# Folding score matrices with heads and key channels on the partitions, and a preparation with its own order

## The chip, the cores and the metric

The kernel runs on one core of a Trainium2 chip. The metric is device time in microseconds (us), the median of several executions; lower is better. The engines have short names: PE is TensorE (matrix products, with PEld for its weight loads), DVE is VectorE, ACT is ScalarE, POOL is GpSimd, SP is SyncE, which here only issues transfers (DMA).

## The reference

Two transformer-like layers on x of shape (8, 512, 256), fp32. Cut to what matters here:

```python
xn = layernorm(x)
q, k, v = split(xn @ Wq.T), split(xn @ Wk.T), split(xn @ Wv.T)      # 16 heads of 64 channels
k, v = concat(mem_k, k), concat(mem_v, v)                           # 64 memory keys in front
dots = einsum('bhid,bhjd->bhij', q, k) * 64 ** -0.5
dots = einsum('bhij,hk->bkij', dots, pre_proj)                      # heads are mixed
...                                          # causal mask; only the 64 largest of a row are kept
attn = einsum('bhij,hk->bkij', softmax(dots), post_proj)
x = x + (attn @ v) @ Wout.T + bout + fp4_ffn(xn)                    # weights and activations rounded to FP4
xn = layernorm(x)
x = x + conv_mlp(xn) + int4_lora_linear(xn)                         # second layer
```

Because the heads are mixed before the softmax, the score of mixed head k between tokens i and j is xn_i times a fixed matrix M_k times xn_j, with M_k = sum over h of pre_proj[h, k] Wq_h^T Wk_h. The kernel computes the 16 matrices M_k (256 x 256 each, and 256 x 64 each for the memory keys) once; this is the fold of the score matrices.

## The kernel before, in words

There are three stages.

**Preparation** (lines 512 to 648, with `prepare`, L240, and `first_guesses`, L378). It loads the weights over two issuing queues (SP and ACT). For each mixed head k it multiplies Wq on DVE with the column pre_proj[:, k] (L587) and runs, for both halves e of the input channels, eight accumulating products over the 1024 inner channels (L593): 16 x 2 x 8 = 256 products, 320 columns each (256 channels and 64 memory keys). ACT copies each result into `mg` and `mgm` (L597, L598) and squares and sums it (L600) for the variance of the scores. `mg` and `mgm` are copied to DRAM. `first_guesses` turns the sums of squares into a first guess of the 64th largest score for each row: a Newton iteration of six rounds, each with a Tanh on ACT (L447) and a chain of small DVE operations. Wv and Wout are transposed. `prepare` rounds the gate, up and down weights of the first layer's MLP to FP4 (steps in `fp4_steps`, L196, that go back and forth between DVE, ACT and POOL; 128 rows of 256 at a time for gate and up, 704 for down), transposes them, and makes the second layer's weights. The results are stored in DRAM (`wgu_d`, `wd_d`, `w1_d`, `bsum_d`). Nobody wrote down an order for this stage: the framework's scheduler picks it, by the place in the program and by readiness.

**The attention loop** (lines 1256 to 1328). The unit is a group: one of the 8 batches and 64 of its 512 tokens; 64 groups. For a batch `tokens` (L687) loads and normalises x and transposes it to `xnT`. `queries` multiplies rows of a pair of groups with `mgm` (L763) and with `mg` (L792); `scores` (L812) multiplies the result with `xnT` (L832) and puts the scores into a place of the ring, a large SBUF buffer with room for four groups. The memory keys' scores go to DRAM and come back in another layout by DMA (L778, L825). `search` (L976) counts in six rounds how many scores of a row lie above a threshold, half on ACT and half on DVE, and starts with a copy of the first guess (L980). Then come the exact 64th value, the exponentials, the head mixing, the product with v and the output projection. All of these operations are added to a `Plan` with an estimated cost and a due time; `Plan.run` (L106) simulates the engines with these costs and emits the instructions in the resulting order[...].

**The second layer** (lines 1377 to 1566), on a batch at a time: parts `norm1`, `convolve`, `norm2` and `finish`, between them the first layer's MLP (`mlp`) of later batches and the rounding of their activations (`quantised`). The framework's scheduler orders this stage, with what comes earlier in the program ahead. Its loop, in short:

```python
for k in range(EARLY, ahead):
    if k not in live and k > b:
        live[k] = quantised(k)
...
(norm1, convolve, norm2, finish)[part](live[b])
```

Of the kernel before, what the change touches and what calls it, by code (L numbers as in the profile page):

```python
# [8 lines left out]
F32 = mybir.dt.float32  # L9
# [57 lines left out]
def keys(ib):  # L67

    return MEM + RB * (ib + 1)


class Op:


    def __init__(self, eng, cost, fn, deps, after, take, give):
        self.eng, self.cost, self.fn, self.deps, self.after = eng, cost, fn, deps, after
        self.take, self.give = take, give
        self.end = self.due = None


class Plan:
# [8 lines left out]
    def add(self, eng, cost, fn, deps=(), take=(), give=(), after=()):  # L90
        op = Op(eng, cost, fn, [d for d in deps if d is not None], [d for d in after if d is not None], take, give)
        if self.room is None:
            fn()
            op.end = 0.0
        else:
            self.ops.append(op)
        return op

# [7 lines left out]
    def run(self, hop=0.1, near=0.08):  # L106
# [13 lines left out]
        while left:  # L120
# [29 lines left out]
            for u in users.get(op, ()):  # L150
                missing[u] -= 1
                if not missing[u]:
                    ready.append(u)

# [85 lines left out]
def prepare(ctx, tc, a, pool, psum, ident, vt, cb, wgu_d, wd_d, w1_d, bsum_d):  # L240

    nc = tc.nc
# [5 lines left out]
    def scratch():  # L248
        return psum.tile([P, 512], F32, name="pps_t")

    with tc.tile_pool(name="pw", bufs=1) as pw:

        vrow = pw.tile([len(VECS), D], F32, name="vrow")
        for i, n in enumerate(VECS):
            (nc.sync, nc.scalar)[i % 2].dma_start(
                vrow[i : i + 1, :], a[f"L1_attn_{n}"].rearrange("(o d) -> o d", o=1)
            )
        ps = scratch()
        for c in range(DC):
            nc.tensor.transpose(  # L260
                ps[:, c * 16 : c * 16 + len(VECS)], vrow[:, c * P : (c + 1) * P], ident[: len(VECS), : len(VECS)]
            )
        nc.vector.tensor_copy(vt, ps[:, : DC * 16].rearrange("p (c v) -> p c v", v=16)[:, :, : len(VECS)])
        for c in range(DC):
            nc.vector.tensor_tensor(cb[:, c : c + 1], vec("Bp", c), vec("Cp", c), ALU.mult)


        wguT = pw.tile([P, DC, 2, FI], F32, name="wguT")
        for u, n in enumerate(("w_gate", "w_up")):
            for r in range(0, FI, P):  # L270
                m = min(P, FI - r)
                w = pool.tile([P, D], F32, name="wrow")
                nc.sync.dma_start(w[:m], a[f"L0_ffn_{n}"][r : r + m, :])
                q = fp4(nc, pool, w[:m], m, D, "w")
                ps = scratch()
                for e in range(DC):
                    nc.tensor.transpose(ps[:, e * P : e * P + m], q[:, e * P : (e + 1) * P], ident[:m, :m])
                nc.scalar.copy(
                    wguT[:, :, u, r : r + m], ps[:, : DC * P].rearrange("p (e m) -> p e m", m=P)[:, :, :m]
                )  # L280
        nc.sync.dma_start(wgu_d, wguT.rearrange("p e u f -> p (e u f)"))
        wdT = pw.tile([P, FKC, D], F32, name="wdT")
        nc.gpsimd.memset(wdT[96:, FKC - 2 :, :], 0.0)
        for o in range(DC):
            w = pw.tile([P, FI], F32, name="wdrow")
            nc.scalar.dma_start(w, a["L0_ffn_w_down"][o * P : (o + 1) * P, :])
            q = fp4(nc, pw, w, P, FI, "d")
            for c0 in range(0, FKC, 3):
                ps = scratch()
                for c in range(c0, c0 + 3):  # L290
                    at, n = FCH[c]
                    nc.tensor.transpose(ps[:n, (c - c0) * P : (c - c0 + 1) * P], q[:, at : at + n], ident)
                for c in range(c0, c0 + 3):
                    at, n = FCH[c]
                    nc.scalar.copy(wdT[:n, c, o * P : (o + 1) * P], ps[:n, (c - c0) * P : (c - c0 + 1) * P])
        nc.sync.dma_start(wd_d, wdT.rearrange("p c d -> p (c d)"))


        w1 = pw.tile([P, 6, DC, D], F32, name="w1")
        for i, n in enumerate(("Wg", "Wi", "Wfg", "Wfu")):  # L300
            (nc.sync, nc.scalar)[i % 2].dma_start(w1[:, i], a[f"L1_attn_{n}"].rearrange("(c p) f -> p c f", p=P))

        for i, n in ((2, "bfg"), (3, "bfu")):
            ps = scratch()
            for o in range(DC):
                for e in range(DC):
                    nc.tensor.matmul(
                        ps[:, o : o + 1], w1[:, i, e, o * P : (o + 1) * P], vec("beta", e),
                        start=(e == 0), stop=(e == DC - 1),
                    )  # L310
            for o in range(DC):
                nc.vector.tensor_tensor(vec(n, o), vec(n, o), ps[:, o : o + 1], ALU.add)
            for e in range(DC):
                nc.vector.tensor_scalar(w1[:, i, e, :], w1[:, i, e, :], vec("gamma", e), None, ALU.mult)

        fd = pw.tile([P, DC, D], F32, name="fd")
        wo1 = pw.tile([P, DC, D], F32, name="wo1")
        nc.sync.dma_start(fd, a["L1_attn_Wfd"].rearrange("(c p) f -> p c f", p=P))
        nc.scalar.dma_start(wo1, a["L1_attn_Wo"].rearrange("(c p) f -> p c f", p=P))
        fdT = pw.tile([P, DC, D], F32, name="fdT")  # L320
        for e in range(DC):
            ps = scratch()
            for c in range(DC):
                nc.tensor.transpose(ps[:, c * P : (c + 1) * P], fd[:, c, e * P : (e + 1) * P], ident)
            nc.scalar.copy(fdT[:, e, :], ps[:, :D])
        for c in range(DC):
            ps = scratch()
            for e in range(DC):
                nc.tensor.matmul(
                    ps[:, :D], fdT[:, e, c * P : (c + 1) * P], wo1[:, e, :], start=(e == 0), stop=(e == DC - 1)  # L330
                )
            nc.scalar.copy(w1[:, 5, c, :], ps[:, :D])
        bfd = pw.tile([P, DC, P], F32, name="bfd")
        for e in range(DC):
            nc.vector.tensor_copy(bfd[:, e, :], vec("bfd", e).to_broadcast([P, P]))
        psb = scratch()
        for e in range(DC):
            nc.tensor.matmul(psb[:, :D], bfd[:, e, :], wo1[:, e, :], start=(e == 0), stop=(e == DC - 1))
        bsum = pw.tile([P, D], F32, name="bsum")
        b1 = pw.tile([P, D], F32, name="b1")  # L340
        nc.sync.dma_start(bsum, a["L1_attn_bo"].partition_broadcast(P))
        nc.scalar.dma_start(b1, a["L1_ffn_bias"].partition_broadcast(P))
        nc.gpsimd.tensor_tensor(bsum, bsum, b1, ALU.add)
        nc.vector.tensor_tensor(bsum, bsum, psb[:, :D], ALU.add)
        nc.sync.dma_start(bsum_d, bsum)

        w4 = pw.tile([P, DC, D], F32, name="w4")
        nc.sync.dma_start(w4, a["L1_ffn_kernel"].rearrange("(c p) f -> p c f", p=P))
        w4f = w4.rearrange("p c f -> p (c f)")
        mx = pw.tile([P, 1], F32, name="mx")  # L350
        nc.vector.tensor_reduce(mx, w4f, AX.X, ALU.max, apply_absolute_value=True)
        mxa = pw.tile([P, 1], F32, name="mxa")
        nc.gpsimd.partition_all_reduce(mxa, mx, P, bass_isa.ReduceOp.max)
        s4 = pw.tile([P, 1], F32, name="s4")
        nc.vector.tensor_scalar(s4, mxa, 1.0 / 7.0, None, ALU.mult)
        r4 = pw.tile([P, 1], F32, name="r4")
        nc.vector.reciprocal(r4, s4)
        nc.vector.tensor_scalar(w4f, w4f, r4, None, ALU.mult)
        nc.vector.tensor_scalar(w4f, w4f, RNE, None, ALU.add)
        nc.vector.tensor_scalar(w4f, w4f, -RNE, None, ALU.add)  # L360
        nc.vector.tensor_scalar(w4f, w4f, 7.0, -8.0, ALU.min, ALU.max)
        nc.vector.tensor_scalar(w4f, w4f, s4, None, ALU.mult)
        la = pw.tile([P, DC, 16], F32, name="la")
        lb = pw.tile([16, D], F32, name="lb")
        nc.sync.dma_start(la, a["L1_ffn_a"].rearrange("(c p) r -> p c r", p=P))
        nc.scalar.dma_start(lb, a["L1_ffn_b"])
        laT = pw.tile([16, DC, P], F32, name="laT")
        for c in range(DC):
            ps = scratch()
            nc.tensor.transpose(ps[:16, :P], la[:, c, :], ident)  # L370
# [1234 lines left out]
```

## Time and profile before

| | us |
|---|---|
| median of 3 runs | 3159.82 (3157.33 to 3160.18) |
| the profiled execution's own time | 3161.28 |
| its span, first to last instruction | 3159.6 |
| PE busy | 2663.9 (84%) |
| DVE busy | 2451.1 (78%) |
| ACT busy | 2052.7 (65%) |
| POOL busy | 1195.4 (38%) |

The page gives for every engine the time that its instructions took. A share is a mean over stages with different limits, so the stages have to be looked at one by one: the profile can be asked for any stretch of time, for the groups of instructions in it (busy time, mean length of one, and the idle time before them with what ended it), for the waits, and for the instructions in order of time. In such a line an arrow `out<-in` names the buffers, `L593` is a line of the kernel, and `[4.74 <-PE x]` after an instruction is the idle time of its engine before it and what ended that. The products are fp32, and each leaves two records in the trace. The mean granted clock of PE was 0.941 of full speed.

### The profile page before, as it was taken

The page shows a single profiled execution, that of the slowest core. Times are in us where ns is not written, and L with a number is a line of the kernel's source. Part 1 is how long each engine was busy: PE and PEld are TensorE (multiplying, and loading weights), DVE is VectorE, ACT ScalarE, POOL GpSimd, SP SyncE. Part 2 cuts the span into 40 slices and gives each one's busy share as a digit, 9 for nine tenths or more (in the row PEclk, how much of TensorE's full clock was granted, in tenths as well). Part 3 has the DMA queues.
Part 4 walks back from the last instruction along what each step waited for, and adds up shares of the span by engine and source line. Part 5 has one row for each costly group of instructions (what it writes and reads, how often), then busy time and mean ns, then how long its engine had stood idle before and what let it go on. Part 6 is the DMA issues. An engine that isn't in the chain of part 4 may idle for free. (4 is left out here: it accounts for less than half of the span.)

```text
span 3159.6 us, 57876 instructions
## 1 busy us (share of the span) xinstructions
PE 2663.9 (84%) x19096; PEld 2033.2 (64%) x19096; DVE 2451.1 (78%) x7973; ACT 2052.7 (65%) x6036; POOL 1195.4 (38%) x2223
## 2 busy tenths in 40 slices
PE   7938889899989989989898998899986558888887
PEld 4726677677768767776776777677664435555554
DVE  5262899989997988899889898979979567776652
ACT  2233878778778877777887787788787334444432
POOL 2030343534534343443434434344445244344330
PEclk9968999999999999999999999999997779999998
DMA  3021000001000100000010000000010110000000
GB/s 109 1 118 49 19 25 17 18 19 30 18 16 18 33 9 26 24 19 16 22 30 16 17 26 17 18 18 26 22 40 5 59 39 20 21 20 14 7 7 13
DMA packets 114152, 82.30 MB, mean 26 GB/s; under 512 B 79131, under 2 KB 108214, under 8 KB 113078
## 3 DMA queue, kind: packets, MB, share of 16 engines
q1 hardware_dynamic: 105548, 66.27, 7.0%
q10 hardware_dynamic: 8298, 12.28, 1.2%
q8 instruction: 153, 2.51, 0.3%
q14 instruction: 153, 1.25, 0.1%
HBM read 43.63 MB, written 34.87 MB: 25 GB/s over the span
## 5 line engine op out<-in xcount | busy, mean ns | idle before, releaser
L874 ACT ACTIVATE junk<-ring,cur 128x312 int8<-128x312 f32 (+26 forms) x1560 | 869.2, 562 | 107.2 <-POOL cur L927 52.7
L878 DVE SCALAR_TENSOR_TENSOR junk<-ring,cur,two 128x72 int8<-128x72 f32 (+10 forms) x1512 | 823.5, 581 | 80.6 <-POOL cur L980 47.0
L832 PE MATMUL ps_sc<-xnT,tk 128*128 128x8 f32 (+38 forms) x2048 | 554.2, 410 | 74.5 <-ACT ring L838 74.2
L792 PEld LDWEIGHTS ps_mi<-rows,mg 128*128 128x128 f32 x4096 | 488.7, 194 | 46.6 <-issue 27.1
L792 PE MATMUL ps_mi<-rows,mg 128*128 128x128 f32 x4096 | 506.8, 278 | 8.5 <-ACT tk L803 4.9
L832 PEld LDWEIGHTS ps_sc<-xnT,tk 128*128 128x128 f32 x2048 | 344.6, 198 | 220.0 <-ACT ring L838 102.8
L1078 PE MATMUL ps_at<-mixd,ring 128*128 128x128 f32 (+1 forms) x3072 | 421.7, 287 | 55.6 <-POOL mixd L1055 33.2
L1078 PEld LDWEIGHTS ps_at<-mixd,ring 128*128 128x128 f32 (+1 forms) x3072 | 379.6, 189 | 97.9 <-POOL mixd L1055 36.0
L962 DVE SCALAR_TENSOR_TENSOR ring<-ring,kth,e 128x520 f32<-128x520 f32 (+56 forms) x512 | 277.3, 559 | 150.4 <-ACT e L953 147.9
L894 POOL TENSOR_TENSOR cur<-base,raw 128x8 f32<-128x8 f32 x186 | 53.1, 286 | 684.3 <-ACT junk L874 671.7
L874 ACT ACTIVATION_READ_ACCUMULATOR junk<-ring,cur 128x1 f32 x1560 | 304.8, 195 | 0.0
L935 DVE SCALAR_TENSOR_TENSOR y<-ring,cur 128x520 f32<-128x520 f32 (+56 forms) x512 | 293.0, 572 | 6.4
L1102 PE MATMUL ps_y<-at,v 128*64 128x64 f32 (+1 forms) x6144 | 224.2, 226 | 78.4 <-ACT at L1084 76.5
L1102 PEld LDWEIGHTS ps_y<-at,v 128*64 128x64 f32 (+1 forms) x6144 | 197.5, 138 | 132.2 <-ACT at L1084 111.2
L938 DVE MAX8 top<-y 128x8 f32<-128x520 f32 (+56 forms) x512 | 255.3, 499 | 17.6
L1084 ACT COPY at<-ps_at 128x512 f32<-128x512 f32 (+1 forms) x384 | 220.8, 579 | 72.5 <-PE ps_at L1078 71.7
L838 ACT COPY ring<-ps_sc 128x456 f32<-128x456 f32 (+56 forms) x512 | 187.9, 373 | 121.1 <-PE ps_sc L832 118.3
L953 ACT ACTIVATE e<-ring 128x520 f32<-128x520 f32 (+56 forms) x512 | 233.0, 474 | 36.2 <-DVE ring L962 34.7
L803 ACT COPY tk<-ps_mi 128x256 f32<-128x256 f32 x512 | 170.6, 371 | 93.2 <-PE ps_mi L792 93.1
L917 POOL TENSOR_TENSOR by<-gap,minus 128x8 f32<-128x8 f32 x124 | 218.9, 1765 | 9.7
L1055 POOL TENSOR_TENSOR mixd<-mix,rden 128x512 f32<-128x512 f32 x128 | 146.8, 1165 | 96.3 <-DVE rden L1047 58.1
L1450 PE MATMUL ps_gu<-mg,xqT 128*128 128x352 f32 x448 | 153.6, 475 | 5.5 <-ACT hid L1454 5.3
(360 smaller groups left out, 4116.8 us busy)
## 6 DMA issues: line engine op xcount, KB each, us to landing
msd<-scr SPq DMA_DIRECT2D x32, 512.0 KB
ring<-msd SPq DMA_DIRECT2D x512, 32.0 KB
scr<-in_L_attn_x_dram SPq DMA_DIRECT2D x9, 512.0 KB
mg_d<-mg SPq DMA_DIRECT2D x1, 4096.0 KB
att<-o SPq DMA_DIRECT2D x64, 64.0 KB
xb<-in_L_attn_x_dram SPq DMA_DIRECT2D x8, 512.0 KB
x<-att ACTq DMA_DIRECT2D x8, 512.0 KB
out_dram<-ob SPq DMA_DIRECT2D x8, 512.0 KB
```

The lines of the kernel that those rows point to most:

```text
L792: nc.tensor.matmul(ps[:, j * P : (j + 1) * P], mg[:, e, k + j, e2 * P : (e2 + 1) * P], toks(e), start=(e == 0), stop=(e == DC - 1),)
L832: nc.tensor.matmul(ps[:, :ntok], q["tk"][side_of(g)][e][:, b].rearrange("p k i -> p (k i)"), o["xnT"][:, e, :ntok], start=(e == 0), stop=( ...
L874: nc.scalar.activation(junk, src, AF.Sign, bias=thr, scale=-1.0, accum_out=raw[:, b : b + 1])
L878: nc.vector.scalar_tensor_tensor(junk, src, thr, two.to_broadcast([P, src.shape[-1]]), ALU.is_ge, ALU.mult, accum_out=raw[:, b : b + 1],)
L917: eng.tensor_tensor(by, gap[:, 1], minus, ALU.pow)
L935: nc.vector.scalar_tensor_tensor(y, src, cur[:, 0, b : b + 1], src, ALU.is_ge, ALU.subtract, reverse1=True)
L938: nc.vector.max(out=top[:, b, :], in_=y)
L953: nc.scalar.activation(e, src, AF.Exp, scale=1.0 / SMALL)
L962: nc.vector.scalar_tensor_tensor(src, src, kth[:, b : b + 1], e, ALU.is_ge, ALU.mult, accum_out=den[:, b : b + 1])
L1078: nc.tensor.matmul(pt[:n, b * P : (b + 1) * P], s[:, 4 * j + b, col : col + n], w["mix"][j][:, b, :], start=True, stop=True,)
L1084: nc.scalar.copy(ats[c][:n, :, j * 4 * RB : (j + 1) * 4 * RB].rearrange("p k (b i) -> p b k i", i=RB), w.pop(("pt", c, j))[:n].rearrange(" ...
L1102: nc.tensor.matmul(w["py"][j * DH : (j + 1) * DH, q * GR : (q + 1) * GR], vs[c][:n, k * DH : (k + 1) * DH], ats[c][:n, k, :], start=(c == ...
```

## The change

It has four parts.

1. **The fold in two steps.** The 256 channels and 64 memory keys are cut into 20 slices of 16. `bd` holds Wk (and the memory keys) in block-diagonal form, so that one product with 32 stationary columns gives, for two heads and 16 key channels, Wq_h^T Wk_h; four such products fill the 128 partitions of a PSUM bank (8 heads by 16 channels), eight both halves of the heads. After a copy to SBUF, a second product with `kr`, which holds pre_proj (scaled) times a 16 x 16 identity pattern, mixes the heads. The squares are taken by ACT on the whole slice and summed in groups of 16 by DVE.
2. **Preparation in an order of its own.** A class `Straight` records each operation of the preparation with an estimated cost and the dependencies found from the memory it touches; `Plan.tails` gives each the length of the longest chain that follows it as its urgency; `Plan.run` writes the order. All loads are issued by SP. Gate and up rows are rounded together (512 columns, six rounds), in two sets of buffers that the down weights use too. The first batch is loaded, normalised and transposed here. Some small constants move into this plan.
3. **First guesses beside the first scores.** Their operations are added to the attention loop's plan, with scratch space in the ring; the searches of the first eight groups and the fourth group's scores wait for them.
4. **Second layer.** In the loop the part of batch b comes before `quantised(k)`.

The core of the diff:

```diff
+    def tails(self):
+        tail = {}
+        for op in reversed(self.ops):
+            op.due = -(tail.get(op, 0.0) + op.cost) + op.late
+            for d in op.deps + op.after:
+                tail[d] = max(tail.get(d, 0.0), tail.get(op, 0.0) + op.cost + 0.1)
...
+        if eng == "PE":
+            return (0.05 + 0.0007 * n) if what == "transpose" else 0.04 + 0.00175 * n
...
-            for k in range(H):
-                wqk = prep2.tile([P, HC, D], F32, name="wqk")
-                nc.vector.tensor_tensor(
-                    wqk, wq, prc[:, :, k : k + 1].to_broadcast([P, HC, D]), ALU.mult
-                )
-                for e in range(DC):
-                    ps = pps.tile([P, 512], F32, name="pps_m")
-                    for c in range(HC):
-                        nc.tensor.matmul(
-                            ps[:, : D + MEM], wqk[:, c, e * P : (e + 1) * P], wkm[:, c, :],
-                            start=(c == 0), stop=(c == HC - 1),
-                        )
-                    nc.scalar.copy(mg[:, e, k, :], ps[:, :D])
-                    nc.scalar.copy(mgm[:, e, k, :], ps[:, D : D + MEM])
...
-            first_guesses(tc, prep, pps, sq, guess, each, far)
...
+            for j in range(NJ):
+                pa = bank("a")
+                for i in range(2):
+                    for u in range(4):
+                        c = 4 * i + u
+                        r.tensor.matmul(
+                            pa[u * 32 : (u + 1) * 32, i * D : (i + 1) * D], bd[:, c, j].rearrange("p t i -> p (t i)"),
+                            wq[:, c, :], start=True, stop=True,
+                        )
+                ab = both[j % 3]
+                r.vector.tensor_copy(ab, pa)
+                pm = bank("m")
+                for e in range(DC):
+                    for i in range(2):
+                        r.tensor.matmul(
+                            pm[:, e * D : (e + 1) * D], ab[:, i * D + e * P : i * D + (e + 1) * P],
+                            kr[:, i].rearrange("p k i -> p (k i)"), start=(i == 0), stop=(i == 1),
+                        )
+                dst = mg[:, :, :, j * 16 : (j + 1) * 16] if j < 16 else mgm[:, :, :, (j - 16) * 16 : (j - 15) * 16]
+                r.scalar.copy(dst, pm.rearrange("p (e k i) -> p e k i", e=DC, i=16))
+                r.scalar.activation(junk[j % 2], pm, AF.Square)
+                r.vector.tensor_reduce(sqp[:, j], junk[j % 2].rearrange("p (q i) -> p q i", i=16), AX.X, ALU.add)
...
+            prepare(r, a, prep, lambda: bank("t"), ident, vt, cb, wgu_d, wd_d, w1_d, bsum_d, wv)
+            r.sync.dma_start(mg_d, mgf)
+            r.sync.dma_start(mgm_d, mgmf)
+            pl.tails()
+            with tc.manual_schedule(engines={nc.tensor.engine, nc.scalar.engine, nc.vector.engine, nc.gpsimd.engine}):
+                pl.run()
...
+        first_guesses(Straight(nc, pl), new, tot, guess, each, far)
+        guessed = pl.add("none", 0.0, lambda: None, list(pl.ops))
+        due(0, 0.0, 0.8)
...
-                o, xdone = tokens(pl, x_in[b])
+                if b == 0:
+                    o, xdone = o0, [pl.add("none", 0.0, lambda: None, (), ["xnT"])]
+                else:
+                    o, xdone = tokens(pl, x_in[b])
...
-            seen = scores(pl, g, s, q, o, qdone, stored)
+            seen = scores(pl, g, s, q, o, qdone, stored, [guessed] * (n == 3))
...
-            tail = search(pl, g, s, w, seen, EDGE if n < 2 else LAST if n > len(groups) - 5 else ROUNDS)
+            tail = search(pl, g, s, w, seen + [guessed] * (n < NG), EDGE if n < 2 else LAST if n > len(groups) - 5 else ROUNDS)
...
+        (norm1, convolve, norm2, finish)[part](live[b])
         for k in range(EARLY, ahead):
             if k not in live and k > b:
                 live[k] = quantised(k)
...
-        (norm1, convolve, norm2, finish)[part](live[b])
```

## The prediction

> **What bounds the kernel now.** I read the span in stretches first: cut where the score fold starts and ends, where preparation ends, at the first search, and where the second layer begins. Columns: stretch, length, busy time and instructions of each engine, granted clock, DMA share, GB/s.
>
> ```profile
> core 0: us, PE busy (x) PEld busy (x) DVE busy (x) ACT busy (x) POOL busy (x), PEclk, DMA share, GB/s
> 0.00:24.00 24.00, 1.08 (x8) 0.93 (x8) 7.00 (x21) 0.00 (x0) 6.07 (x124) 1.00 0.77 219
> 24.00:166.00 142.00, 140.49 (x514) 98.65 (x515) 52.95 (x72) 47.30 (x205) 15.66 (x14) 1.00 0.09 28
> 166.00:222.00 56.00, 11.84 (x63) 7.57 (x64) 48.81 (x201) 18.78 (x45) 21.20 (x31) 0.58 0.24 98
> 222.00:255.00 33.00, 14.27 (x58) 10.97 (x56) 13.06 (x45) 6.16 (x20) 4.19 (x6) 0.60 0.39 151
> 255.00:302.00 47.00, 47.00 (x259) 33.69 (x259) 0.26 (x1) 16.58 (x41) 1.27 (x4) 0.97 0.16 46
> 302.00:2512.00 2210.00, 1954.88 (x16395) 1565.22 (x16393) 1928.39 (x6926) 1711.51 (x5296) 921.98 (x1924) 0.96 0.07 20
> 2512.00:2557.00 45.00, 0.00 (x0) 0.00 (x0) 20.23 (x45) 10.17 (x19) 20.22 (x10) 0.52 0.47 158
> 2557.00:3159.60 602.60, 494.29 (x1808) 316.18 (x1808) 380.36 (x665) 242.24 (x411) 204.79 (x114) 0.92 0.04 14
> ```
>
> Before 302 us the engines work one after another: loads, then TensorE alone for 142 us, then VectorE alone for 56 us (weight rounding and first guesses), then a 33 us remainder with a token norm, then TensorE alone again while VectorE has 0.26 us of work. From 302 us the loop has PE and DVE at 87 to 88%; the change doesn't touch its instructions. So the gain is read from the front.
>
> Next the groups and waits of those stretches, and single records of the time order, for prices:
>
> ```profile
> L593 PE MATMUL pps_m<-wkm,wqk 128*128 128x320 f32 x512 | 140.3, 438 | 0.8 <-DVE wkm L581 0.8
> DVE junk L878 <- POOL cur L980: 47.0, 1, 47.0
> 254.96 3.15 PE L721 MATMUL ps_mi<-wvT,xnT 128*128 128x512 f32 x4
> 257.95 3.60 PE L763 MATMUL ps_mi<-mgm,rows 128*128 128x512 f32 x8
> 603.69 1.15 PE L1102 MATMUL ps_y<-at,v 128*64 128x64 f32 x32 [3.27 <-ACT at L1084]
> 23.38 0.69 DVE L581 COPY wkm<-pps_t 128x512 f32<-128x512 f32 x1 [0.32 <-PE pps_t L576]
> 39.84 0.68 DVE L351 TENSOR_REDUCE mx<-w 128x1 f32<-128x512 f32 x1
> 166.29 0.23 DVE L393 COPY fg_tot<-pps_t 128x64 f32<-128x64 f32 x1 [16.75 <-PE pps_t L391]
> 215.62 0.21 DVE L464 TENSOR_TENSOR guess<-guess,fg_f 128x64 f32<-128x64 f32 x1
> 2539.27 2.06 ACT L191 ACTIVATE xn<-x,ln_mr,ln_ri 128x256 f32<-128x256 f32 x4
> 2557.24 1.97 PE L1404 MATMUL ps_tr<-ident,q_lo_x 128*128 128x128 f32 x8 [46.19 <-POOL q_lo_x L226]
> ```
>
> The fold never waits, so its matmuls are the bound there. The first search waits 47 us on its begin, which waits for scores. The loop's first product (values of batch 0) is at 255 us; call its start T0.
>
> [...] The trace has only two-tile work, L1102: (1.15 - 0.22)/31 = 0.030 us a record of 64 columns, against 0.054 us at the full-array rate of L763 (3.60/8 = 0.45, some 0.43 in steady state, for 512 columns). So neighbours overlap, nearly two at a time. [...] Each fp32 product here leaves two records (512 for the 256 products of L593)[...]. [...] The trace, with both in use, moved 219 GB/s in the first 24 us; so I give loads from SP alone that rate. [...]
>
> **The change part by part.**
>
> *The fold.* Removed: 256 products of 320 columns, 16 scalings of 2.29 us on DVE, and on ACT 32 times (0.37 + 0.22 + 0.42 + 0.19 + 0.26 + 0.19). Added, for each of 20 slices of 16 key channels: eight products of 32 stationary and 256 moving columns, four of 128 and 256; a DVE copy of 512 from PSUM (0.69) and a sum of 512 (0.68); an ACT copy (0.58) and square (about 0.65). A full 256-column product is two records of 0.215, 0.43 us. Second step: 80 x 0.43 = 34 us. First step: 160 x 0.43 = 69 us without overlap, 17 with four tiles, 34 if only the second pass of one tile overlaps the first of the next. I take 34[...]. So 68 us, with ends of 51 and 103, where 142 were.
>
> *The other PE work of preparation* stays: some 92 transposes at 0.115 (L611: 16 in 1.92) are 11 us; the small products of the last part (3.4 + 3.0 + 1.0 + 1.9) are 9. PE in all: 88 us.
>
> *DVE.* Slices: 20 x 1.37 = 27. Weight rounding: gate and up rows now go together, 512 wide, in six rounds, down in two. From the 704-wide records (0.88, 0.19, 0.43, four of 0.53, two of 0.89: 5.4) a 512-wide round is 4.2. 6 x 4.2 + 2 x 5.4 = 36. Gate/up evictions move to DVE: 6 x 0.69 = 4. Block-diagonal fill 6, token norm 4, the fourth layer's weights and masks 10. Sum 87, and 8 more for operations that stretch while POOL runs (L219: 0.29 alone, 1.48 beside POOL). ACT has about 52 and POOL 35; neither ends last.
>
> *When.* K and Q weights, 2.1 MB at 219 GB/s, plus about 2 us: products start near 12.5 us instead of 24. PE alone ends at 12.5 + 88 = 101; DVE, from 7 us with the fill, at 7 + 95 = 102. The two interlock in order (a fold copy stands behind rounding operations, and the order was planned with a price of 0.04 + 0.00175 x 256 = 0.49 us a product, 5.9 a slice, with no overlap). For that I estimate 10 us, 0 to 20; and 3 us from the last slice to the total of squares. T0 = 115. Saved: 255 - 115 = 140 us. The batch's load, norm, transposes and the wait for the L1 weights' store (DVE 5.5 us before L161) lie inside.
>
> *DMA.* All loads go to SP, ACT is freed. The large copy of the score matrices to DRAM (5.2 MB, 24 us at that rate) is issued once they are complete; until T0 + 24 it lies ahead of the memory columns' round trip, which is needed only before the search at T0 + 47. Nothing, or 5 us if late.
>
> *First guesses.* They leave preparation and stand on DVE ahead of the first search. One of six iterations is 18 operations, 4.9 us of records, and a Tanh of 0.31 with handoffs: 5.4. Six and a preamble of 5 make 37 us; before, mixed with rounding, 49 (166.3 to 215.6). The cover is the 47 us of scores in which DVE was idle. I count 0; at the old 49 us pace it shows 2 to 5 us. Without that cover it would cost all 37. Queued behind it on DVE is only the first search; the fourth group's scores also wait for it (shared ring space), some 20 us later.
>
> *Second layer.* norm1 of the first batch comes ahead of rounding of the second. PE stood 46 us; the first batch's normalised tokens were there at 2541.3, but their transposes stood behind those of the rounded ones at 2557. So about 9 us of PE work (transposes 1.8, first projections 7) can come earlier, and rounding of batch two is put back 2 to 3 us by norm work on DVE and ACT. PE is 82% busy after that, so I take -5, bounds -12 and +8.
>
> *The loop* is re-planned by the same cost list. No instruction of it changes; 0, within 12 either way.
>
> Sum: 3161.3 - 140 + 0 - 5 + 0 = 3016 for the profiled execution, which lies 1.5 above the median of the runs shown. Prediction: 3015.
>
> **The rivals.**
>
> 1. *Column tiles do not overlap.* For: [...]four tiles were never seen here. Against: L1102. Then PE needs 103 + 20 = 123 us from 12.5, interlock falls to 5: T0 = 141, time 3041.
>
> 2. *Four overlap, and VectorE alone bounds preparation.* For: PE's fold falls to 51 us. T0 is 102 + 3 = 105, second layer at its -12: 2998; with less of the stretching on DVE, 2990.
>
> 3. *Slower: the re-planned loop loses pace.* Place: the order written for L1328. Price: 2210/64 = 34.5 us a group; it decides at 145/64 = 2.3 us more a group (36.8). For: the order is fixed by estimated costs, and the added dependency of eight searches shifts its start. Against: after the first groups the same due times rule. At 37.1 the time is 3180.
>
> 4. *The gain is partly given back early.* Guesses or the memory columns come late, or preparation's order stalls PE on rounding (PE waited 43 us for POOL's L226 between 166 and 255): T0 near 165, time 3065 and up.
>
> That the change doesn't do what it says would leave 3160; the 142 us of L593 can't stay, so only a fold of equal cost could do it.
>
> **How the numbers follow.** My forecast 0.50 (own range 3000 to 3031), rival 1 0.22 (3031 to 3052), rival 2 0.15 (2980 to 3000), rival 4 0.09, rival 3 0.03, no change 0.01. The range 2984 to 3052 leaves out rivals 3 and 4, no change and the lowest part of rival 2, some 0.16 of the chance. Slower by over 0.2%: rival 3 and the far end of rival 4, 0.04; within 0.2%: 0.01; faster by over 0.2%: the rest, 0.95. A difference of 0.2% is about what a measurement of this kernel can tell from none.
>
> **What would show it.** First products near 12 us; a slice pitch on PE of 3.4 us where nothing delays it (5.2 for rival 1, 2.6 for rival 2); the first query product at 115 us; the guess finished about 40 us later, before the first search near 162; the loop from there to the last out-projection still 2205 to 2215 us; in the second layer, transposes of the first batch ahead of the rounded ones. I am wrong if the loop's length moves by more than 15 us, or if PE waits for rounding in preparation by more than 20.

## The result, and the profile after

The changed kernel takes 3037.9 us (median of four runs, 3035.61 to 3044.78) against 3158.57 us (3152.27 to 3160.18): a ratio of 0.9625, 95% interval 0.9604 to 0.9646. That is 23 us above the forecast of 3015 and inside its range. Its profiled execution took 3036.97 us, with a span of 3035.3.

The same cuts as before, moved to where the stages of the changed kernel begin: fold 9.7 to 79.5, the rest of preparation to the loop's first product (T0), the first scores, the loop to the end of its products, the stretch in which PE stands, and the second layer. Columns as before: stretch, length, busy time and instructions of each engine, granted clock, DMA share, GB/s.

```profile
core 0: us, PE busy (x) PEld busy (x) DVE busy (x) ACT busy (x) POOL busy (x), PEclk, DMA share, GB/s
0.00:9.70 9.70, 1.09 (x8) 0.94 (x9) 7.96 (x16) 3.10 (x4) 7.45 (x119) 1.00 0.88 226
9.70:79.50 69.80, 61.40 (x482) 40.98 (x483) 45.69 (x88) 27.42 (x50) 10.40 (x9) 0.95 0.38 122
79.50:151.10 71.60, 24.68 (x120) 19.02 (x118) 35.77 (x79) 15.80 (x36) 22.03 (x17) 0.59 0.27 101
151.10:201.20 50.10, 48.67 (x257) 33.87 (x258) 32.21 (x140) 18.91 (x49) 3.64 (x15) 0.93 0.20 64
2397.00:2425.00 28.00, 0.07 (x1) 0.07 (x2) 8.42 (x33) 2.79 (x6) 11.82 (x6) 0.58 0.57 201
```

The fold went from 142 us to 69.8. But the 71.6 us after it hold only 24.7 us of PE work, 35.8 of DVE and 22.0 of POOL: no engine is full there. The order in time on PE says what it waits for (start, length, operation, count; in brackets the idle time before it and what ended that):

```profile
46.72 1.93 PE L230 MATMUL pps<-wq,bd 128*32 128x256 f32 x32
48.58 3.72 PE L230 MATMUL pps<-kr,both 128*128 128x256 f32 x16
52.23 1.93 PE L230 MATMUL pps<-wq,bd 128*32 128x256 f32 x32
...
86.89 1.06 PE L230 MATMUL pps<-ident,w_lo 128*128 128x128 f32 x8 [0.19 <-ACT woT L230]
94.91 2.13 PE L230 MATMUL pps<-ident,w_lo 128*128 128x128 f32 x8 [6.95 <-POOL w_lo L230]
118.18 1.73 PE L230 MATMUL pps<-ident,w_lo 128*128 128x128 f32 x8 [21.14 <-POOL w_lo L230]
134.75 1.54 PE L230 MATMUL pps<-ident,w_lo 128*128 128x128 f32 x6 [14.84 <-POOL w_lo L230]
...
151.09 3.09 PE L896 MATMUL ps_mi<-wvT,xnT 128*128 128x512 f32 x4 [0.52 <-DVE w1s L230]
```

Two things are to be seen. The first step of two slices (32 records) takes 1.93 us, 0.06 us a record, and two slices follow each other every 5.5 us. And the transposes of rounded weights (`w_lo`) come only after the fold, with three waits for rounding, 42.9 us in all. In the kernel before, PE waited 49.2 us for rounded weights (43.0 in ten waits for the gate and up rows, 6.2 for the down rows): the change shortened the fold and left most of the waits.

The first search starts at 201.23 us (302.06 before). The first guesses ended just ahead of it. Their last operation on DVE, and POOL's order in time:

```profile
199.20 0.19 DVE L230 TENSOR_SCALAR far<-ring 128x64 f32<-128x64 f32 x1
198.06 0.47 POOL L990 MEMSET ring<- 128x392 f32 x1 [22.50 <-DVE ring L230]
198.50 0.30 POOL L1029 TENSOR_TENSOR ring<-ring,cmask 128x56 f32<-128x56 f32 x1
201.08 0.20 POOL L1031 TENSOR_TENSOR ring<-ring,cmask 128x8 f32<-128x8 f32 x1 [2.28 <-ACT ring L1013]
201.23 0.19 POOL L1155 COPY cur<-guess 128x8 f32<-128x8 f32 x1
```

POOL got on at 198.06, when DVE was done with the part of the ring that POOL clears there, and then waited another 2.28 us for scores; DVE's last operation for the guesses ended at 199.39, some 2 us before these scores. In the second layer, PE stood 28 us where it had stood 46, and the first batch's transposes and projections now come ahead of the rounded activations:

```profile
2424.93 2.17 PE L1598 MATMUL ps_tr<-ident,xn 128*128 128x128 f32 x8 [28.11 <-ACT xn L299]
2427.56 9.29 PE L1606 MATMUL ps_l<-xn1T,w 128*128 128x512 f32 x16 [0.46 <-ACT xn1T L1599]
...
2447.84 1.97 PE L1598 MATMUL ps_tr<-ident,q_lo_x 128*128 128x128 f32 x8 [4.99 <-POOL q_lo_x L334]
```

The whole difference of 124.3 us in span, read at three marks: the first search begins 100.8 us earlier; from there to the last product of the loop's stage it is 13.4 us less (2192.8 for 2206.2); the rest is 10.1 us less (641.2 for 651.3). The 13.4 us of the middle part go for the most part with the granted clock and not with the change: the trace shows the same instructions in the same order there, and the length times the mean granted clock of that part, taken from the trace's clock records, is 2206.2 x 0.964 = 2126 us before and 2192.8 x 0.968 = 2123 after.

### The profile page after: what moved, and what is told of

The parts are those of the page before. It is cut to its first block, busy times and chain, and to the rows that moved or that the text cites. A ratio compares the mean times of both kernels' runs of the same rounds, so it can differ in the third digit from the quotient of the medians.

```text
span 3035.3 us, 57571 instructions
## 1 busy us (share of the span) xinstructions
PE 2587.1 (85%) x19064; PEld 1978.8 (65%) x19064; DVE 2453.7 (81%) x7958; ACT 2028.2 (67%) x5862; POOL 1190.0 (39%) x2206
```

## The experiments

Each kernel is the changed one with one edit or a few, but for the fold alone, which is the kernel before with the new fold. T0 is the start of the loop's first product, S0 that of the first search; "loop" is from S0 to the last product of the loop's stage, "rest" from there to the end. "Rounding" is what PE waited for rounded weights before T0. All times are of the profiled execution; the ratio is of medians to the kernel before.

| kernel | rounding | T0 | S0 | loop | rest | span | ratio (95%) |
|---|---|---|---|---|---|---|---|
| before | 49.2 | 255.0 | 302.1 | 2206.2 | 651.3 | 3159.6 | 1 |
| fold alone | 48.9 | 203.6 | 251.2 | 2201.5 | 649.6 | 3102.3 | 0.9841 (0.9817 to 0.9864) |
| changed | 42.9 | 151.1 | 201.2 | 2192.8 | 641.2 | 3035.3 | 0.9625 (0.9604 to 0.9646) |
| changed, once more | 43.0 | 153.0 | 203.7 | 2198.5 | 639.5 | 3041.7 | 0.9625 (0.9609 to 0.9641) |
| guesses in preparation | 52.1 | 160.4 | 215.1 | 2205.7 | 638.5 | 3059.3 | 0.9683 (0.9661 to 0.9706) |
| old second layer | 43.1 | 149.8 | 198.4 | 2201.0 | 653.7 | 3053.1 | 0.9698 (0.9674 to 0.9722) |
| other bank | 18.4 | 131.0 | 181.2 | 2192.7 | 643.7 | 3017.6 | 0.9564 (0.9548 to 0.9580) |
| more urgent | 42.9 | 170.2 | 221.0 | 2198.7 | 638.7 | 3058.4 | 0.9682 (0.9666 to 0.9698) |
| measured prices | 43.8 | 140.8 | 190.9 | 2192.9 | 637.8 | 3021.6 | 0.9571 (0.9547 to 0.9595) |
| bank and urgency -60 | 9.1 | 142.7 | 188.5 | 2191.7 | 641.3 | 3021.5 | 0.9565 (0.9539 to 0.9591) |
| bank and urgency -10 | 4.4 | 127.2 | 174.7 | 2204.6 | 638.3 | 3017.6 | 0.9570 (0.9554 to 0.9586) |
| bank, -10 and prices | 1.6 | 128.8 | 174.6 | 2200.2 | 639.3 | 3014.1 | 0.9519 (0.9496 to 0.9541) |

### What keeps rounding behind the fold: the bank of one small product

The transposes of preparation take three PSUM banks in turn (`bank("t")`), and so does one product behind the fold, the total of squares. Whatever takes its bank next has the whole fold among its ancestors in the list. One edit gives that product a bank of the second step:

```diff
-            ps = bank("t")
+            ps = bank("m")
             r.tensor.matmul(ps[:, : 2 * DC * H], ones, sq.rearrange("p i q -> p (i q)"), start=True, stop=True)
```

> One change to the changed kernel: the total of squares gets a PSUM bank of the fold's own set instead of one of the three banks that all the transposes use in turn. Theory: in the changed kernel the gate and up transposes wait behind that total, hence behind the whole fold, because they need its bank, and with them the two sets of rounding buffers; freed of it, rounding runs beside the fold, the loop's first product comes at about 115 us instead of 151, and the time is about 3002 us (2992 to 3015). Rival: preparation is bound by the chain of rounding operations across DVE, ACT and POOL itself; then rounding beside the fold only stretches both, the first product stays at 140 us or later and the time at 3028 or more.

T0 is at 131.0 us, 20 earlier, and the time 3020.9 us: between the theory (115, 3002) and its rival (140 or later, 3028 or more). The transposes of rounded rows now stand inside the fold, on PE's order in time:

```profile
56.45 0.60 PE L230 MATMUL pps<-ident,w_lo 128*128 128x128 f32 x4
56.98 1.07 PE L230 MATMUL pps<-wq,bd 128*32 128x256 f32 x16
57.99 0.66 PE L230 MATMUL pps<-ident,w_lo 128*128 128x128 f32 x4
58.57 1.07 PE L230 MATMUL pps<-wq,bd 128*32 128x256 f32 x16
```

What PE still waited for, in the view of waits up to T0 (engine, buffer and line, releaser: us in total, times, longest):

```profile
PE pps L230 <- POOL w_lo L230: 18.4, 3, 14.6
PE pps L230 <- DVE both L230: 14.2, 8, 5.4
```

So the bank cost 24.5 us of waiting for rounding, of which 6.6 came back as waits of the fold for DVE (14.2 for 7.6). That the shared bank was a cause is shown; that it was the only one is not, since 14.6 us of waiting for the down weights stayed: their rounding starts on DVE at 102.53 us, behind the last operations of the fold.

### The order alone

The list has a constant by which everything after the fold is less urgent. Here it is made much more urgent, with the old bank and with the new one:

```diff
-            r.late = 4.0
+            r.late = -60.0
```

> One change to the changed kernel: everything after the fold in preparation gets an urgency 64 us higher, the banks stay. Theory (the shared bank): the transposes of rounded weights still need the total of squares first, so nothing moves by more than 6 us: 3032 to 3044. Rival (only the list's urgency keeps them behind the fold): the first product comes 20 to 36 us earlier, 3002 to 3018.

> Both changes: the bank of its own and the higher urgency. Rounding and transposes then go ahead of most of the fold, and the total of squares comes last. Theory: about as good as the bank alone in the first product (110 to 120 us), but the guesses, which need the total, start late and the first search may wait for them: 3000 to 3015. Rival (rounding's own chain bounds preparation): 3028 or more.

Neither came as expected. With the old bank it costs 19 us (T0 170.2), where the theory allowed 6. Rounding still stands behind the fold (42.9 us of waits), and the fold itself starts at 16.6 us and is soon held up: PE waited 14.55 us for DVE's copy of a slice, because DVE's order had the maximum of the gate and up rows ahead of it, and that waited for its load. DVE in order of time:

```profile
24.05 0.69 DVE L230 TENSOR_REDUCE w_amax<-w_v 128x32 f32<-128x512 f32 x1 [3.49 <-DMA w_v<-in_L_ffn_w_up_dram]
...
32.91 0.69 DVE L230 TENSOR_REDUCE w_amax<-w_v 128x32 f32<-128x512 f32 x1 [7.50 <-DMA w_v<-in_L_ffn_w_up_dram]
...
34.05 0.69 DVE L230 COPY both<-pps 128x512 f32<-128x512 f32 x1
```

With the new bank the waits for rounding fall to 9.1 us, but the fold runs from 21 to 139 us and ends last: T0 is 142.7, not the 110 to 120 expected. Its S0 is only 45.8 us after T0, not 50.1. PE's wait of 1.4 us for POOL's first copy is gone (in the changed kernel that copy stood behind a wait for the store of the second layer's weights). The rest goes with the granted clock, 1.00 in this stretch against 0.93: PE's busy time times the clock is 45.8 us here (45.77 x 1.00) and 45.3 there (48.67 x 0.93). Fold first or rounding first, DVE is idle for a third of the time to T0 or more (89 us of work in 151, 92 in 143).

### The price of a product

The order is planned with 0.49 us for each product of the fold, of either step. The measured prices are put in, 0.12 and 0.43 (other products of preparation get the second formula too):

```diff
+        if what == "matmul":
+            n = ins[1].shape[-1]
+            cost = 0.12 if out.shape[0] == 32 else 0.03 + 0.00156 * n
```

> One change to the changed kernel: the list is given the measured prices of the products, 0.12 us for one of the first step and 0.43 for one of the second, instead of 0.49 for both. Theory (the shared bank): the order of PE stays fold first, and the time within 6 us of the changed kernel's: 3032 to 3044. Rival (the wrong price spoils the order): 3010 or less.

I had expected almost nothing; the time is between theory and rival. The ratio is 0.9571, T0 140.8, 10.3 us earlier: fold products run from 9.7 to 68 us instead of 79.5. The waits show how: none of PE's 7.6 us of waits for DVE's copies is left in the fold, while the waits for rounding are all there (43.8 us). DVE still rounds within the fold (from 25 us on), but the copies of slices now stand between these operations in time; in the changed kernel ten operations of rounding in a row came between the copies at 18.61 and 24.41 us.

### The three together, and two of them

The new bank and an urgency of -10 (14 more than in the changed kernel), without and with the measured prices:

```diff
-            ps = bank("t")
+            ps = bank("m")
...
-            r.late = 4.0
+            r.late = -10.0
```

> The other bank and the urgency, but the old prices. If the order of the down weights against the fold's end is what the run with the other bank alone still lacked, the first product moves from 131 to some 118 to 124 us and the time is 3004 to 3012; if the prices matter as much (the fold is then planned at 5.9 us a slice and leaves holes), it stays at 126 or later and the time is 3012 to 3020.

> All three small edits of preparation's list at once: the total of squares in a bank that the transposes do not use, the prices of the products as measured (0.12 us for one of 32 stationary columns, 0.43 for a full one of 256), and everything after the fold made more urgent by 14 us, so that the down weights are rounded before the fold's last slices. My theory (the shared bank and the wrong price kept rounding and the fold apart, nothing else stood between the changed kernel and the start that I had put at 115 us): waits of TensorE for rounded weights before the loop fall from 43 us to under 15, the loop's first product is at 115 us (108 to 123), the first search 46 us later because the loop's weights are stored in good time, at 161; with the loop and second layer as in the changed kernel the time is 2997 (2988 to 3008). Rival (VectorE and GpSimd share what limits rounding, so an order cannot gain more than the shared bank alone did): first product at 128 to 135, time 3015 to 3022.

> The changed kernel once more, unaltered, beside the two above. First product at 151 us, first search at 201, as in its first record. From the first search to the last product of the loop 2192.8 us if that length belongs to the program; if it belongs to the execution (two kernels with the same order of the loop took 2199 and 2201), anything from 2191 to 2202, and then the 13 us by which the loop came out shorter than before are not all the change's.

The waits for rounding are nearly gone in both (4.4 and 1.6 us), and T0 is at 127.2 and 128.8. For the kernel with all three, T0 is where the rival put it, and the time, 3008 us, at the upper end of the theory's. For the other, T0 stayed at 126 or later, which I had tied to the old prices; but with the measured ones it is no earlier. The edits are worth 22 to 24 us at T0, and 115 was not reached. What stands in the place of rounding, for the kernel with all three up to T0:

```profile
PE pps L233 <- DVE scr L233: 20.3, 2, 19.1
PE pps L233 <- DVE bd L233: 11.8, 1, 11.8
PE pps L233 <- DVE both L233: 6.8, 3, 4.0
...
PE pps L233 <- POOL w_lo L233: 1.6, 1, 1.6
```

Here PE's first work, transposes of the first batch, comes at 19 us, and the first product of the fold at 44, because the filling of `bd` is queued on DVE behind rounding that waits for loads (8.2 us at one place). From 44 to 129 us PE and DVE work side by side, 87% and 78% busy. DVE has 92.5 us of work before T0, PE 84.5. So the order that would start the fold at 10 us and lose no wait was not found; that one exists is not shown.

The kernel with all three is the fastest tried: 3008.35 us (3002.63 to 3015.88), 0.9519 (0.9496 to 0.9541). That the prices add to the other two edits isn't shown: S0 is at 174.6 and 174.7 us in the two, and the 13 us between their medians come with different granted clocks (0.946 to 0.953 in its four runs, 0.940 to 0.943 in those without the prices).

The changed kernel once more gave T0 153.0, S0 203.7 and 2198.5 us from there to the last product of the loop, for 2192.8: that length belongs to the execution, not to the program alone. With 149.8 us for the same preparation in the kernel with the old second layer, differences of 3 us in T0 say nothing.

### The four column tiles

Two edits ask what makes the first step so fast. In the first, products that use the same tile stand next to each other:

```diff
-                for i in range(2):
-                    for u in range(4):
+                for u in range(4):
+                    for i in range(2):
```

> The changed kernel with the eight first-step products of a slice in another order: two that use the same column tile stand next to each other. If products start in program order and both passes of one hold its tile (my assumption in the prediction), a slice's first step goes from the 0.93 us measured to 1.7 us or more. If each tile takes its products by itself, it stays at 0.9 to 1.0 us.

In the second, eight products more are put into the first tile of every slice, with a result that was there already:

```diff
+                for i in range(8):
+                    r.tensor.matmul(
+                        pa[0:32, (i % 2) * D : (i % 2 + 1) * D], bd[:, 4 * (i % 2), j].rearrange("p t i -> p (t i)"),
+                        wq[:, 4 * (i % 2), :], start=True, stop=True,
+                    )
```

> The changed kernel with eight more products in each of the 20 slices, all eight in the first of the four column tiles; they write again what the first product of each half of the heads wrote, so the result is the same. In the changed kernel eight products spread over four tiles took 0.97 us a slice (16 records of 0.06), about a quarter of the full-array rate of 0.23 a record. If that comes from four tiles working side by side, eight in one tile take four times as long, 3.4 to 3.7 us more a slice: first and second step of two slices together go from 5.5 us to about 12.5, and the fold ends some 65 to 75 us later. If a product of 32 stationary columns is itself that short and the tiles take turns, the eight take 0.97 us more a slice, two slices go to about 7.5 us and the fold ends about 20 us later.

PE's order in time with same-tile neighbours:

```profile
49.90 1.97 PE L230 MATMUL pps<-wq,bd 128*32 128x256 f32 x32
51.80 3.72 PE L230 MATMUL pps<-kr,both 128*128 128x256 f32 x16
55.45 1.97 PE L230 MATMUL pps<-wq,bd 128*32 128x256 f32 x32
```

and with the eight extra products in one tile:

```profile
60.80 8.82 PE L230 MATMUL pps<-wq,bd 128*32 128x256 f32 x64
69.55 3.72 PE L230 MATMUL pps<-kr,both 128*128 128x256 f32 x16
73.20 8.82 PE L230 MATMUL pps<-wq,bd 128*32 128x256 f32 x64
```

32 more records in one tile cost 8.82 - 1.93 = 6.89 us, 0.215 us each, close to the 0.233 of a full-array record of the second step (3.72/16); spread over four tiles a record costs 0.060. So the tiles do work side by side, and the speed isn't that of a narrow product by itself. (Each of these two kernels has one run.) And the order inside a slice doesn't matter (1.97 for 1.93 us; the kernel's time was 3041.7 us, its span 3040.0): four records in a row on one tile take 0.86 us at 0.215, yet a slice's 16 take 0.985, so the next tile's products didn't wait until the four of the first tile were done. Single records show the same: the first four of a slice start within 0.04 us of each other and the next four some 0.2 us later, although in the program four records of the first tile stand ahead of the second tile's first. The extra products lengthened the fold by 60.9 us (65 to 75 expected; PE's waits for DVE's copies fell from 7.6 to 2.1) and the span by 64.3, to 3099.6.

### The other three parts

The new fold alone, in the kernel before, with the old order, loads, guesses and second layer:

```diff
-            for k in range(H):
-                wqk = prep2.tile([P, HC, D], F32, name="wqk")
...
+            for j in range(NJ):
+                pa = pps.tile([P, 512], F32, name="pps_m")
```

> The kernel before with the new fold alone, in the framework's own order, with guesses in preparation and the old order of the second layer. Theory: the fold takes 55 to 60 us of PE instead of 142, while the rounding that was hidden beside it comes out: the loop's first product at 170 to 190 us instead of 255, time 3075 to 3095. Rival (nearly all of the gain is the fold, the planned order adds nothing): 3055 or less. Rival (the gain is the order): 3120 or more.

It gains 1.6%, and less than expected. The fold takes 20.4 to 111.2 us. PE's order in time shows one slice every 4 us or so, since in the written order the second step waits for DVE's copy of its own slice (21.8 us in all):

```profile
62.09 1.97 PE L616 MATMUL pps_m<-kr,both 128*128 128x256 f32 x8 [0.90 <-DVE both L612]
63.99 1.07 PE L607 MATMUL pps_m<-wq,bd 128*32 128x256 f32 x16
66.64 1.97 PE L616 MATMUL pps_m<-kr,both 128*128 128x256 f32 x8 [1.58 <-DVE both L612]
```

So the rest of the change has its part: from this T0 to the changed kernel's are 52.5 us. There the fold starts 10.7 us earlier and is 21 us shorter (69.8 for 90.8), 11.2 us of PE's idle time before the first batch's transposes are gone, and the waits for rounding are 6 us less.

The first guesses put back into preparation, with scratch in `bd`, and no search waiting for them in the loop's plan:

```diff
-        first_guesses(Straight(nc, pl), new, tot, guess, each, far)
-        guessed = pl.add("none", 0.0, lambda: None, list(pl.ops))
+        guessed = None
...
+            first_guesses(r, new, tot, guess, each, far)
             prepare(r, a, prep, lambda: bank("t"), ident, vt, cb, wgu_d, wd_d, w1_d, bsum_d, wv)
```

> The changed kernel with the first guesses back in preparation, planned with it. Theory: preparation has VectorE idle for some 25 us between 85 and 150 us, so the guesses' 37 us come out partly: first product 5 to 15 us later, time 3043 to 3055. Rival (they were the cover's only use and cost their full length): 3070 or more. Rival (they cost nothing in either place): 3034 to 3041.

T0 is 9.3 us later, as expected, and S0 13.8: 9.2 us more of waiting for rounding, since the guesses take DVE's time there, and 6.2 us (1.4 in the changed kernel) of waiting for POOL's copy of rows behind the end of the guesses. The median is 1.5 us above the expected range.

The second group's search starts 18.06 us after the first, 13.15 in the changed kernel. Only some 1.3 us of that can come with the guesses' place, for in the fold alone, which has them in preparation too, it is 14.47 us. The rest goes with the granted clock of that stretch (last but two in a line), for the kernel before (17.36 us), the fold alone, guesses in preparation and the changed kernel; PE's busy time times the clock is 13.0 to 13.2 us in all four:

```profile
302.00:319.50 17.50, 16.20 (x96) 14.42 (x95) 11.42 (x38) 14.22 (x43) 1.23 (x6) 0.80 0.00 1
251.00:265.70 14.70, 13.22 (x97) 11.34 (x96) 11.20 (x38) 14.41 (x43) 1.59 (x5) 1.00 0.01 1
215.00:233.10 18.10, 16.07 (x97) 14.40 (x96) 11.19 (x38) 14.38 (x43) 1.64 (x5) 0.81 0.00 0
201.20:214.40 13.20, 13.00 (x97) 11.20 (x96) 11.22 (x38) 12.92 (x42) 1.44 (x6) 1.00 0.00 1
```

And the old order of the second layer:

```diff
-        (norm1, convolve, norm2, finish)[part](live[b])
         for k in range(EARLY, ahead):
...
+        (norm1, convolve, norm2, finish)[part](live[b])
```

> The changed kernel with the old order in the second layer's loop. Theory: the second layer, from the last product of the first layer's MLP to the end, is again 651 us long instead of 641: 3048 (3042 to 3053). Rival (the 10 us come from elsewhere): 3035 to 3041.

Its first record after the loop:

```profile
2449.56 1.97 PE L1598 MATMUL ps_tr<-ident,q_lo_x 128*128 128x128 f32 x8 [47.36 <-POOL q_lo_x L334]
```

The rest is 653.7 us, against 637.8 to 643.7 in the nine tabled kernels with the new order: the swap is worth 10 to 16 us. The granted clock doesn't explain that: it was 0.889 in this part, and 0.882 to 0.889 in those nine. The medians differ by more (0.9698 against 0.9625, 23 us of 3155; 3059 us, where I expected 3042 to 3053); of the 17.8 us in span, 8.2 are in the loop, whose order this kernel doesn't change.

## Why the prediction was right, and where not

The time lay in the range, the sign and the order of size were right, but not by the likeliest case as I had put it, and in part by luck: 3037.9 us is in the stretch that I had given to rival 1, whose cause is ruled out below. By its steps:

1. **First step of the fold, "34 if only the second pass of one tile overlaps the first of the next. I take 34".** Measured 22.9 us busy, 19.3 at the steady 0.97 us a slice. Four tiles overlap: 0.060 us a record against 0.233 of the second step (3.72/16) is 3.9 times, and 3.6 times against the 0.215 of a record in one tile. The half overlap that I took was my estimate, which no trace had shown; it fell with the run that puts same-tile products side by side, 0.985 us a slice where it asked for 1.7 or more.
2. **Second step, 34.** Measured 39.7. PE was busy for 61.4 us of the fold and waited 8.9 for copies and loads (the records overlap a little), so it took 69.8 us, where I had 68: errors that cancel. Where nothing delays it, a slice follows the last after 2.76 us (5.51 for two), nearer the 2.6 that I gave as rival 2's sign than my 3.4.
3. **Start at 12.5, other PE work 20.** The start was mis-added, 2.1 MB at 219 GB/s and 2 us are 11.6; measured 9.7, with loads at 226 GB/s from one issuing queue. Behind the fold, 28.7 us (71.6 - 42.9) weren't waits for rounding, 24.7 of them PE's work, at a granted clock of 0.59 in that stretch.
4. **DVE 95 us before T0.** Measured 89.4.
5. **"The two interlock in order ... I estimate 10 us, 0 to 20."** This is the step that failed: 50.5 us in place of 10. PE waited 42.9 us for rounding after the fold and 7.6 for copies within it. I had named it as the mark of a wrong prediction (more than 20 us), had the kernel before's 43 us in the text as evidence for rival 4, and gave that 0.09. I had looked at how much work each engine has, not at who is whose ancestor in the list; the bank that one small product shares with the transposes put rounding behind the fold, as the run with the other bank shows. That bank accounts for 24.5 us of the waits; the rest is in part the order of the down weights against the fold's end, and no run shows that all of it could be avoided.
6. **T0 115, saved 140.** From its terms: 9.7 + 69.8 + 42.9 + 28.7 = 151.1, saved 103.9.
7. **First guesses at nothing.** Right: S0 follows T0 by 50.1 us (47.1 before). Of the 3 us more, 1.4 are PE's wait for POOL's first copy of rows, which stood behind a wait for the store of the second layer's weights; the rest goes with the granted clock (PE busy 48.7 us at 0.93, before 47.0 at 0.97). The guesses ended some 2 us before the scores. Without the cover they cost 13.8 us, not 37: preparation has room on DVE.
8. **Second layer -5.** Measured -10.1, and 10 to 16 with the run that undoes it: the mechanism was right (first batch's transposes ahead of the rounded ones), the size too small. PE stood 18 us less, not 9.
9. **Loop 0, within 12.** Measured -13.4, and the loop missed the 2205 to 2215 us that I had given as a sign. That isn't the work of the loop, which is the same: length times granted clock is 2126 us before and 2123 after. Whether the change has a part in the clock isn't shown. Eleven records of kernels with the guesses in the loop lie between 2191.7 and 2204.6 us, with a mean of 2196.7; the kernel before and the fold alone, with the same order in the loop, have 2206.2 and 2201.5.

The sum: 3161.3 - 103.9 + 3.0 - 13.4 - 10.1 = 3036.9. Of the 36 us by which T0 was missed, the loop and the second layer gave back 18.5. Without these the time would have been 3056 us, outside the range. The 5.1 from the second layer are the forecast's own mechanism, larger than I put it; most of the loop's 13.4 goes with the clock, of which the forecast said nothing: luck.

Rival 1 (no overlap) is ruled out by the extra products in one tile. Rival 2 was right that four tiles overlap, not that VectorE is then full: it works 89 of 151 us. Rival 3 didn't occur. Rival 4 named the right wait; its price, T0 at 165, was 14 us too high.

## What to carry to other kernels

A sum of busy times says when preparation could end; what decides is who waits for whom in the planned order, so follow one late buffer back through the banks and buffers that it shares, a small last product among them. When a stage is shortened, look at the waits beside it in the trace of before: 49 us for rounding were there, and 43 were there again after. Give a planner the measured price of a new kind of instruction: here that alone brought the loop 10 us forward, but nothing more once the bank and the urgency were changed. And before a difference of some microseconds is explained by the program, compare length times granted clock.

## What the hardware showed that I had not expected

- Products of 32 stationary columns in four column tiles run side by side, in both orders within a slice that were tried: 0.060 and 0.062 us a record spread, 0.215 in one tile.
- The loop's instructions, in the same order, take 2191.7 to 2206.2 us in the fourteen profiles, that of the kernel before included. Length times mean granted clock (0.962 to 0.970) is 2120 to 2127 us in all of them, so what differs is mostly the clock. Why the clock differs isn't shown.
- The times of whole executions move with the clock less strictly: the four runs of the kernel with all three edits had 0.946, 0.946, 0.951 and 0.953 of full speed and took 3015.9, 3013.6, 3002.6 and 3003.1 us, but with the bank and an urgency of -60, 0.945 took 3019.5 and 0.946 took 3030.4. So a single profile tells nothing of a few microseconds in the loop.
